# A mixture of experts inside a four-stage kernel: all experts for two blocks, and for six blocks rows sorted by expert and moved by indirect DMA

## The chip, the cores and the metric

The kernel runs on one core of a Trainium2 chip. The metric is the device time of one launch in microseconds. A core has a matrix engine (TensorE, PE in the profile; its weight loads are listed as PEld), a vector engine (VectorE, DVE), an activation engine (ScalarE, ACT), a general engine (GpSimd, POOL) and a queue that issues transfers (SyncE, SP). Each engine works through its own list of instructions in order.

## The reference

The input is four sequences of 1024 rows of 128 numbers. Four stages follow each other; each adds to `x` the layernorm of what it computed from the layernorm of `x`: a state-space scan ("mamba"), a mixture of experts, a windowed convolution whose 31 weights are computed per row and head, and a transformer of six layers with attention over windows of 32 rows. The stage that changes is the second:

```python
def _L0_ffn_ref(x, w_router, w_up, b_up, w_down, b_down):
    K = 2
    logits = jnp.einsum('bsd,ed->bse', x, w_router)
    top_logits, idx = jax.lax.top_k(logits, K)
    router_weights = jax.nn.softmax(top_logits, axis=-1)
    h = jnp.einsum('eud,bsd->bseu', w_up, x) + b_up[None, None]
    h = jax.nn.gelu(h, approximate=False)
    y = jnp.einsum('edu,bseu->bsed', w_down, h) + b_down[None, None]
    y_k = jnp.take_along_axis(y, idx[..., None], axis=2)
    out = jnp.einsum('bskd,bsk->bsd', y_k, router_weights)
    return out
```

There are eight experts of 512 hidden units. Every row needs only the two experts with the largest logits, a quarter of what the formula computes. Everything is in f32.

## The kernel before

The rows are worked in eight blocks of 512 (two to a sequence), `x[k]` for block k. `mamba(k)`, `moe(k)` and `conv(k)` prepare a block; the transformer takes a sequence in tiles of 128 rows, 4 sequences x 6 layers x 8 tiles = 192 tiles, numbered through.

`moe` (line 669) normalises a block, transposes it to `xT`, computes the logits, and finds the two best experts by reductions and comparisons on small tiles (`lg`, `hot`, `best`, `gates`), so that `gates` holds the weight of each of the eight experts, zero for six of them. Then it goes through 16 pairs of half a block and expert (`sub` outside, `e` inside). For each it loads the expert's up and down weights (`ewup`, `ewdn`, 256 KB each, from SP), multiplies up (`up`: four matmuls of 256 columns into two banks, Gelu by ACT), and one step later down (`down`: eight matmuls of 128 columns), multiplies the result by the gate (`eye`, DVE) and adds it to `eacc` (POOL). So all experts are computed for all rows, and the weights of a block are loaded twice.

The order of the instructions is made by the kernel itself. The stages are generators that record units of work (`Order.take`, line 164), with yields that say how much was recorded. `Transformer.run` (line 1268) records the tiles one after the other and, between their parts, advances two lines of side jobs: experts (lines 1295 and 1296) and others, mamba and conv (lines 1297 to 1300). An entry such as `(E, 3, 23, 36)` means the experts of block 3 are recorded from tile 23 to tile 36. Blocks 0 and 1 are recorded ahead of the transformer by `merge` (line 422). Then `Order.arrange` (line 267) gives out the units: for each engine it takes, among the units whose inputs its own table of durations (`length`, line 240) says are there, those that can start within a small margin (`NEAR`, line 147) and of them the one recorded first; it looks at most 500 units ahead and hands out seven PSUM banks. `Order.give` (line 344) issues them, which is why nearly every record of the profile has its line, L349. The hardware runs each engine's list in that order, with semaphores for what is not ready.

SP's list holds all transfers, POOL's none. On SP the rotary tables (`rot`, one per tile, three buffers), the transformer's weights and the expert weights follow each other. On POOL stand the rotary additions `r<-r,rb`, the multiplications `r<-r,root` and `at<-at,sm`, the adds of mamba and conv, and `eacc`.

Buffers are rings of a fixed number (`Rings`, line 379). Two that the change touches: `hs` (the transformer's state, two tiles `hs0` and `hs1`, each with two buffers, line 897) and `fxT` in `feedforward` (line 1218), which has its own buffer.

Of the kernel before, what the change touches and what calls it, by code (L numbers as in the profile page):

```python
# [24 lines left out]
NEXP, UP = 8, 512  # L25
NUC = UP // P
# [6 lines left out]
SUB = 256  # L33
# [23 lines left out]
class Late:  # L57
# [13 lines left out]
    def rearrange(self, *a, **k):  # L71
        return self.then(lambda ap: ap.rearrange(*a, **k))

# [66 lines left out]
class Order:  # L140
# [23 lines left out]
    def take(self, engine, op, args, kw):  # L164
        out = kw.get("out", args[0] if args else None)
        ins = [a for a in list(args) + list(kw.values()) if a is not out]
        ins = [a for a in ins if isinstance(a, (Late, bass.AP))]
# [72 lines left out]
    def length(self, engine, op, out, ins, kw):  # L240
# [17 lines left out]
        if engine == "scalar":  # L258
            return 0.25 + n * (0.45e-3 if n <= 512 else 0.7e-3), 0.12
        if op in ("tensor_copy", "memset"):  # L260
            return 0.15 + n * 1.0e-3, 0.08
# [139 lines left out]
@with_exitstack  # L401
def sandwich(ctx: ExitStack, tc: tile.TileContext, io: dict, out: bass.AP):


    c = Common(ctx, tc, io, out)
    t = Transformer(ctx, c)
    prepare = t.prepare()
    for _ in c.mamba(0):
        next(prepare, None)
    merge([(c.mamba(1), MAMBA), (c.moe(0), MOE), (prepare, 2.0 * DEPTH)])  # L410
    merge([(c.conv(0), CONV), (c.moe(1), MOE)])
    t.run()
    c.nc.arrange()
    with tc.manual_schedule():
        c.nc.give()
# [3 lines left out]
MAMBA, MOE, CONV = 60.0, 64.0, 59.0  # L419
# [15 lines left out]
class Common:  # L435


    def __init__(self, ctx, tc, io, out):
# [11 lines left out]
        self.rows = [dram.tile([PADL + SEQ, D], F32, name=f"rows{b}") for b in range(NB)]  # L450

# [18 lines left out]
        self.bup = const.tile([P, NEXP, NUC], F32, name="bup")  # L470
        self.bdn = const.tile([NEXP, D], F32, name="bdn")
        self.wl = const.tile([P, CH * CK], F32, name="wl")
        for t, k in (
# [5 lines left out]
            (self.bup, "b_upT"),  # L479
            (self.bdn, "b_dn"),  # L480
            (self.wl, "w_linT"),
        ):
# [15 lines left out]
        zero = const.tile([PADL, D], F32, name="zero")  # L498
        nc.gpsimd.memset(zero, 0.0)
        for rows in self.rows:  # L500
            dma(out=rows[:PADL, :], in_=zero)
# [167 lines left out]
    def moe(self, k):  # L669
        nc, dma, io = self.nc, self.dma, self.io  # L670
        x = self.x[k]
        full, row = [P, 4, NEXP], [P, 4]
        size = {
            "wup": ([P, UP], 2), "wdn": ([P, NUC, D], 3), "hg": ([P, 2, SUB], 4),
            "ye": ([P, 2, D], 2), "xT": ([P, BLK], 1), "acc": ([P, 4, D], 1),
            "gT": ([P, BLK], 1), "lg": (full, 1), "gates": (full, 1), "hot0": (full, 1),
            "hot1": (full, 1), "top": ([P, 2, 4], 1), "best": (row, 1), "ed": (row, 1),
            "wgt": ([P, 2, 4], 1),
        }

        def tile(name):
            shape, bufs = size[name]
            tag = "xn" if name == "gT" else name
            return self.sb.tile(shape, F32, name, tag="e" + tag, bufs=bufs)

        def weights(i):
            e = i % NEXP
            wup, wdn = tile("wup"), tile("wdn")
            dma(out=wup, in_=io["w_upT"][:, e, :])
            dma(out=wdn, in_=io["w_dnT"][:, e, :, :])  # L690
            return wup, wdn

        ahead = [weights(0)]
        xT = tile("xT")
        xn = self.norm(x, "e", "exn")
        yield 4
        nc.scalar.copy(xT, self.turned(xn, "e"))
        yield 2


        pl = self.bank("pl")[:, : 4 * NEXP].rearrange("p (t e) -> p t e", e=NEXP)
        with nc.together(0.9):
            for t in range(4):
                nc.tensor.matmul(
                    pl[:, t, :], xT[:, t * P : (t + 1) * P], self.wr, start=True, stop=True
                )
        lg, gates, top, best = tile("lg"), tile("gates"), tile("top"), tile("best")
        hot = [tile("hot0"), tile("hot1")]
        rank = self.rank[:, None, :].to_broadcast(full)
        nc.vector.tensor_copy(lg, pl)  # L710
        for i in range(2):
# [9 lines left out]
            if i == 0:  # L721
# [3 lines left out]
                nc.vector.tensor_tensor(out=lg, in0=lg, in1=gates, op=ALU.min)  # L725

        ed, wgt = tile("ed"), tile("wgt")
# [5 lines left out]
        for i in range(2):  # L733
            nc.vector.tensor_tensor(
                out=hot[i], in0=hot[i], in1=wgt[:, i, :, None].to_broadcast(full), op=ALU.mult
            )
        nc.vector.tensor_tensor(out=gates, in0=hot[0], in1=hot[1], op=ALU.add)
        yield 6


        acc = tile("acc")

        def biases():
            gT = tile("gT")
            ps = self.transpose4("gTp", [gates[:, g, :] for g in range(4)])
            nc.scalar.copy(gT[:NEXP], ps[:NEXP].rearrange("p g f -> p (g f)"))
            yield 2
            pa = self.bank("pacc").rearrange("p (g f) -> p g f", g=4)
            with nc.together(0.9):
                for g in range(4):  # L750
                    nc.tensor.matmul(
                        pa[:, g, :], gT[:NEXP, g * P : (g + 1) * P], self.bdn, start=True, stop=True
                    )
            nc.scalar.copy(acc, pa)
            yield 2

        def up(e, sub, wup):
            hg = []
            for i in range(NUC // 2):
                pu = self.bank("pu").rearrange("p (u f) -> p u f", u=2)  # L760
                h = tile("hg")
                with nc.together(0.88):
                    for u in range(2):
# [3 lines left out]
                            wup[:, uc * P : (uc + 1) * P],  # L767
# [706 lines left out]
```

## Time and profile before

| | |
|---|---|
| median of three runs | 4319.4 us (4319.16 to 4320.47) |
| profiled execution | 4318.73 us, its span 4316.9 us |
| mean granted TensorE clock | 0.965 |
| PE, DVE, ACT, POOL busy | 3947.9, 3714.9, 2672.7, 2867.3 us |
| DMA | 264.55 MB, mean 61 GB/s |
| expert weight loads | 256 of 256 KB |

A row of a group reads: line, engine, operation, output and input by the program's names, shapes, count, then the busy time and the mean of one record, then the idle time of the engine just before them and what ended most of it. Busy times of PE are unions of overlapping records, so the mean of one record is longer than its share of the busy time; an f32 matmul leaves two records, a transpose and a bf16 matmul one. The span falls into a start (0 to about 330 us, blocks 0 and 1 before the first transformer tile), a long middle in which transformer tiles and side jobs mix, and an end from about 3450 us in which the transformer is alone. The expert matmuls of blocks 2 to 7 lie between 648 and 3238 us.

### The profile page before, as it was taken

What the parts mean: (1) busy time and instruction counts of PE and PEld (TensorE: products, weight loads), DVE (VectorE), ACT (ScalarE), POOL (GpSimd) and SP (SyncE); (2) the same over time, 40 slices, a digit from 0 to 9 for tenths busy, and PEclk for the clock granted to TensorE, in tenths of its full rate; (3) what the DMA queues carried; (4) which work ended last, traced back from release to release, by engine and by line L of the source; (5) the groups of instructions that cost most, each with busy time, mean ns of one, the idle gap of its engine ahead of it and who ended that gap; (6) DMA issues with size and microseconds to landing.
All of it is one profiled execution on the core that took longest, in us unless ns stands there. A gap on an engine that the chain in (4) does not pass through costs nothing. (4 is left out here: it accounts for less than half of the span.)

```text
span 4316.9 us, 114247 instructions
## 1 busy us (share of the span) xinstructions
PE 3947.9 (91%) x46400; PEld 2883.0 (67%) x46400; DVE 3714.9 (86%) x9520; ACT 2672.7 (62%) x4666; POOL 2867.3 (66%) x1760
## 2 busy tenths in 40 slices
PE   5665789999999999899999999999999999999997
PEld 2553456776666777677766767677767677777775
DVE  5537799988899899998999989988889989989986
ACT  4443557666765676567756677566765566666664
POOL 4467656658668666696668666578558766666663
PEclk7887899999999999999999999999999999999999
DMA  5542001122112111121111211121111111001010
GB/s 173 193 151 83 28 29 37 62 80 92 60 65 75 48 52 50 57 92 56 47 60 66 68 44 44 63 82 53 54 63 56 46 33 34 30 24 34 25 34 11
DMA packets 127223, 264.55 MB, mean 61 GB/s; under 512 B 14384, under 2 KB 66792, under 8 KB 118760
## 3 DMA queue, kind: packets, MB, share of 16 engines
q1 hardware_dynamic: 126696, 257.25, 17.9%
q8 instruction: 365, 5.98, 0.6%
q14 instruction: 162, 1.33, 0.1%
HBM read 238.26 MB, written 18.94 MB: 60 GB/s over the span
## 5 line engine op out<-in xcount | busy, mean ns | idle before, releaser
L349 POOL TENSOR_TENSOR r<-r,rb 128x1024 f32<-128x1024 f32 x384 | 905.8, 2362 | 446.7 <-DVE rb L349 357.8
L349 POOL TENSOR_TENSOR r<-r,root 128x1024 f32<-128x1024 f32 x384 | 723.2, 1904 | 225.2 <-DVE root L349 192.2
L349 PEld LDWEIGHTS bank<-zT,wvo 128*128 128x128 f32 x6144 | 716.4, 192 | 100.2 <-issue 54.5
L349 PE MATMUL bank<-wqk,hs 128*128 128x512 f32 x1536 | 743.7, 614 | 33.9 <-DVE at L349 11.8
L349 PE MATMUL bank<-zT,wvo 128*128 128x128 f32 x6144 | 722.3, 276 | 9.8 <-ACT zT L349 6.9
L349 ACT ACTIVATE sq<-bank 128x512 f32<-128x512 f32 x768 | 439.7, 599 | 356.5 <-PE bank L349 133.1
L349 ACT COPY zT<-bank 128x512 f32<-128x512 f32 x768 | 401.0, 597 | 340.2 <-PE bank L349 339.5
L349 POOL TENSOR_TENSOR at<-at,sm 128x1024 f32<-128x1024 f32 x192 | 365.5, 1904 | 347.6 <-DVE sm L349 200.3
L349 DVE TENSOR_TENSOR r<-bank,rot 128x512 f32<-128x512 f32 x768 | 523.7, 682 | 74.3 <-PE bank L349 28.6
L349 DVE TENSOR_TENSOR rb<-bank,rot 128x512 f32<-128x512 f32 x768 | 524.3, 683 | 48.1 <-ACT sq L349 46.4
L349 DVE TENSOR_REDUCE words<-sq 128x8 f32<-128x512 f32 x768 | 527.6, 687 | 5.9
L349 PEld LDWEIGHTS bank<-wqk,hs 128*128 128x128 f32 x1536 | 273.8, 193 | 322.4 <-issue 191.5
L349 PE MATMUL bank<-ident,r 128*128 128x128 f32 x3072 | 394.5, 278 | 52.3 <-POOL r L349 18.3
L349 PE MATMUL bank<-aT,xw 64*128 64x256 f32 x3072 | 426.2, 399 | 16.7 <-DVE at L349 6.8
L349 PEld LDWEIGHTS bank<-ident,r 128*128 128x128 f32 x3072 | 349.5, 143 | 119.6 <-issue 43.3
L349 PEld LDWEIGHTS bank<-aT,xw 64*128 64x128 f32 x3072 | 296.1, 189 | 142.5 <-issue 54.4
L349 ACT ACT_TABLE_LOAD x264 | 338.7, 1283 | 28.0 <-DVE ne L349 10.4
L349 ACT COPY qT<-bank 128x512 f32<-128x512 f32 x384 | 228.1, 596 | 192.2 <-PE bank L349 188.7
L349 PEld LDWEIGHTS bank<-kT,qT 64*32 64x32 f32 x24576 | 254.9, 105 | 85.7 <-issue 83.1
L349 DVE TENSOR_REDUCE mx<-bank 128x8 f32<-128x512 f32 x384 | 254.2, 682 | 50.1 <-PE bank L349 49.8
L349 PE MATMUL bank<-exT,ewup 128*128 128x256 f32 x1024 | 270.3, 399 | 26.9 <-DVE near L349 11.0
L349 PE MATMUL bank<-kT,qT 64*32 64x64 f32 x24576 | 286.4, 226 | 0.6 <-issue 0.6
(148 smaller groups left out, 7155.5 us busy)
## 6 DMA issues: line engine op xcount, KB each, us to landing
ewup<-in_w_upT SPq DMA_DIRECT2D x128, 256.0 KB
ewdn<-in_w_dnT SPq DMA_DIRECT2D x128, 256.0 KB
near<-rows SPq DMA_DIRECT2D x32, 1024.0 KB
near<-rows SPq DMA_DIRECT2D x32, 960.0 KB
rot<-rotd SPq DMA_DIRECT2D x192, 128.0 KB
wqk<-in_Wqkv SPq DMA_DIRECT2D x48, 512.0 KB
wvo<-wvod SPq DMA_DIRECT2D x24, 1024.0 KB
w<-in_W SPq DMA_DIRECT2D x24, 341.0 KB
```

Of the source, the lines that this page charges most:

```text
L349: getattr(engine, op)(*map(real, args), **{k: real(v) for k, v in kw.items()})
```

## The change

Blocks 0 and 1 keep all experts, in `all_experts`: the expert outside and the half block inside, so that a weight tile is loaded once per block; up weights, down weights and the bias lie in one row of `w_ex` (4112 bytes per partition, 526 KB per expert), with three buffers and two loads ahead.

Blocks 2 to 7 are taken by sequence, two blocks at a time, in `chosen_experts`. After the same routing (now `route`, for one or two blocks), a matmul with a triangle of ones counts for every row how many earlier rows chose the same expert; from this follow each row's two places in a list sorted by expert, in which each expert begins at a multiple of 128, and the expert of each of the list's 23 tiles (16 full ones and up to seven part-filled). 16 indirect DMAs, issued by POOL, write the normalised rows to a DRAM list (`listed`); each list is zeroed once at the start. For each tile POOL fetches that expert's weights by an indirect DMA, SP loads the 128 rows; PE transposes them, multiplies up and down; ACT copies the result out and SP stores it to `results`. At the end POOL fetches each row's two results by indirect DMAs (16), and DVE adds them with their weights to the bias term, which stays in a PSUM bank. In the built program POOL so issues 48 scatters, 69 weight fetches and 48 gathers, each scatter waiting for the one before; ACT's list holds 173 table loads, before 264.

The side jobs are placed anew. `indirect_dma_start` gets an entry in the table of durations. To make room, `hs1` has one buffer, and `fxT` shares that of `fxn`.

```diff
-    merge([(c.mamba(1), MAMBA), (c.moe(0), MOE), (prepare, 2.0 * DEPTH)])
-    merge([(c.conv(0), CONV), (c.moe(1), MOE)])
+    merge([(c.mamba(1), MAMBA), (c.all_experts(0), ALL), (prepare, 2.0 * DEPTH)])
+    merge([(c.conv(0), CONV), (c.all_experts(1), ALL)])
...
+        for listed in self.listed:
+            dma(
+                out=listed.rearrange("(i p) d -> p i d", p=P),
+                in_=zero[:, None, :].to_broadcast([P, MAXT, D]),
+            )
...
+    def all_experts(self, k):
+        def weights(e):
+            w = self.sb.tile([P, 2 * UP + NUC], F32, "ewt", bufs=3)
+            dma(out=w, in_=self.io["w_ex"][e * P : (e + 1) * P, :])
+            return w
+        ahead = [weights(0), weights(1)]
...
         for i in range(2 * NEXP):
-            sub, e = divmod(i, NEXP)
+            e, sub = divmod(i, 2)
...
+    def chosen_experts(self, ks):
+        n = 4 * len(ks)
+        nt = 2 * n + NEXP - 1
...
+        yield from self.route(ks)
+        xn, _, lg, hot, gates, wgt = self.routed
+        nc.vector.tensor_tensor(out=hots, in0=hot[0], in1=hot[1], op=ALU.add)
...
+            nc.tensor.matmul(
+                count[:, :w], self.tri, flat, start=True, stop=False, skip_group_check=True
+            )
+            for t in range(1, n):
+                nc.tensor.matmul(
+                    count[:, t * NEXP : w],
+                    self.ones,
+                    flat[:, : w - t * NEXP],
...
+        for t in range(n):
+            for i in range(2):
+                nc.gpsimd.indirect_dma_start(
+                    out=listed[:, :],
+                    out_offset=at(idx[:, i, t : t + 1]),
+                    in_=xn[:, t, :],
+                    in_offset=None,
+                )
+                yield 1
+
+        def fetch(i):
+            w = self.sb.tile([P, 2 * UP + NUC], F32, "ewt", bufs=3)
+            nc.gpsimd.indirect_dma_start(
+                out=w, out_offset=None, in_=self.io["w_ex"], in_offset=at(widx[:, i : i + 1])
+            )
+            xs = self.sb.tile([P, D], F32, "exs", bufs=2)
+            dma(out=xs, in_=listed[i * P : (i + 1) * P, :])
+            return w, xs
+
+        def down(i, w, hg):
+            pd = self.bank("pdn")[:, :D]
...
+            ye = self.sb.tile([P, 2, D], F32, "ey", bufs=3)[:, 0, :]
+            nc.scalar.copy(ye, pd)
+            dma(out=results[i * P : (i + 1) * P, :], in_=ye)
+
+        ahead = [fetch(0), fetch(1)]
+        last = None
+        for i in range(nt):
+            w, xs = ahead.pop(0)
+            px = self.bank("pxs")[:, :P]
+            nc.tensor.transpose(px, xs, self.ident)
+            xT = self.sb.tile([P, P], F32, "exsT", bufs=2)
+            nc.scalar.copy(xT, px)
...
+            if last:
+                down(*last)
+            last = i, w, hg
+            if i + 2 < nt:
+                ahead.append(fetch(i + 2))
...
+        for i, k in enumerate(ks):
+            yield from self.biases(i, self.sb.tile([P, BLK], F32, "eT"), gates)
+            acc = self.biased
+            for g in range(4):
+                t = 4 * i + g
+                for j in range(2):
+                    yk = self.sb.tile([P, 2, D], F32, "ey", bufs=3)[:, 0, :]
+                    nc.gpsimd.indirect_dma_start(
+                        out=yk, out_offset=None, in_=results[:, :], in_offset=at(idx[:, j, t : t + 1])
+                    )
+                    nc.vector.scalar_tensor_tensor(
+                        acc[:, g, :], yk, wgt[:, j, t : t + 1], acc[:, g, :], ALU.mult, ALU.add
+                    )
+            yn = xn[:, :4, :]
+            self.layernorm(yn, acc, 4)
...
-                self.sb.tile([P, COLS], F32, f"hs{i}", bufs=2) for i in range(2)
+                self.sb.tile([P, COLS], F32, f"hs{i}", bufs=2 - i) for i in range(2)
...
-        xT = self.sb.tile([P, BLK], F32, "fxT")
+        xT = self.sb.tile([P, BLK], F32, "fxT", tag="fxn")
...
-        experts = [(E, 2, 10, 23), (E, 3, 23, 36), (E, 4, 36, 60), (E, 5, 60, 80)]
-        experts += [(E, 6, 80, 106), (E, 7, 106, 128)]
-        others = [(C, 1, 0, 2.6), (M, 2, 2.6, 10), (M, 3, 10, 20), (C, 2, 23, 30)]
-        others += [(M, 4, 30, 36), (C, 3, 36, 45), (M, 5, 46, 60), (C, 4, 60, 70)]
-        others += [(M, 6, 70, 80), (C, 5, 80, 93), (M, 7, 93, 106), (C, 6, 106, 124)]
-        others += [(C, 7, 128, 142)]
+        experts = [(E, (2, 3), 18, 30), (E, (4, 5), 56, 78), (E, (6, 7), 84, 118)]
+        others = [(C, 1, 0, 2.6), (M, 2, 2.6, 11), (M, 3, 11, 18), (M, 4, 18, 30)]
+        others += [(C, 2, 30, 38), (C, 3, 38, 46), (M, 5, 46, 56), (M, 6, 56, 67)]
+        others += [(M, 7, 67, 78), (C, 4, 78, 87), (C, 5, 87, 97), (C, 6, 118, 130)]
+        others += [(C, 7, 130, 144)]
```

## The prediction

> **What bounds the kernel now.** I read the totals first, then the busy times by stretch, then the groups of the stretch that the change touches, and then the waits. The totals say that two engines are nearly full together, TensorE before VectorE.
>
> ```profile
> span 4316.9 us, 114247 instructions
> ...
> PE 3947.9 (91%) x46400; PEld 2883.0 (67%) x46400; DVE 3714.9 (86%) x9520; ACT 2672.7 (62%) x4666; POOL 2867.3 (66%) x1760
> ...
> PE 3%; DVE 1%; ACT 0%; issue 0%; POOL 0%; POOLq 0%; ACTq 0%; DVEq 0%
> ```
>
> The chain that ended last reaches back only 4% of the span, so it covers the tail and says nothing about the middle. The stretches do (columns: stretch, length, then busy us and instruction count of PE, PEld, DVE, ACT, POOL; granted clock, DMA share, GB/s):
>
> ```profile
> 540.00:755.00 215.00, 196.78 (x2179) 136.03 (x2179) 203.02 (x491) 136.04 (x236) 135.02 (x85) 0.96 0.11 33
> 755.00:971.00 216.00, 208.68 (x2514) 161.62 (x2513) 190.73 (x493) 143.17 (x252) 128.74 (x83) 1.00 0.21 71
> ...
> 1187.00:1403.00 216.00, 197.87 (x2186) 140.12 (x2186) 203.38 (x512) 127.63 (x222) 156.66 (x91) 0.94 0.21 70
> ...
> 3454.00:4209.00 755.00, 748.82 (x10031) 549.70 (x10020) 682.21 (x1751) 462.74 (x806) 478.75 (x271) 1.00 0.10 30
> ```
>
> The last line is the transformer alone: PE 99%, a PE bound; 92 `mx` reductions, two a tile, lie in it, so 46 tiles at 16.4 us. The second has experts beside it: PE 97%, DVE 88%. The first and third have mamba and almost no experts: DVE 94%, PE 91.5%, clock 0.94 to 0.96, so there DVE is the fuller one. The six expert blocks that change all lie in 540 to 3200 us:
>
> ```profile
> 540.00:3200.00 2660.00, 2541.19 (x29806) 1866.20 (x29806) 2400.81 (x6137) 1771.73 (x3063) 1822.77 (x1123) 0.99 0.18 59
> ```
>
> In it PE is 95.5% busy and DVE 90.3%: together 1.858 of two engines. POOL has 837 us idle and ACT 888. Groups of that stretch (busy us, mean ns, then idle before them):
>
> ```profile
> L349 ACT ACT_TABLE_LOAD x206 | 264.3, 1283 | 24.2 <-DVE ne L349 10.4 <-DVE at L349 9.6 <-DVE rs L349 0.6
> L349 PE MATMUL bank<-exT,ewup 128*128 128x256 f32 x768 | 202.0, 392 | 9.3 <-DVE at L349 6.1 <-ACT zT L349 1.8 <-DVE hs L349 0.8
> L349 PE MATMUL bank<-ewdn,ehg 128*128 128x128 f32 x1536 | 191.1, 278 | 1.6 <-ACT ehg L349 1.2 <-DVE rb L349 0.4
> L349 ACT ACTIVATE ehg<-bank,bup 128x256 f32<-128x256 f32 x384 | 159.3, 477 | 53.6 <-PE bank L349 50.4 <-DVE mx L349 1.3
> ...
> L349 POOL TENSOR_TENSOR eacc<-eacc,eye 128x256 f32<-128x256 f32 x96 | 69.9, 728 | 45.8 <-DVE eye L349 24.8 <-DVE ne L349 13.1 <-DVE words L349 4.2
> L349 DVE TENSOR_TENSOR eye<-bank,egates 128x256 f32<-128x256 f32 x96 | 40.3, 420 | 37.1 <-PE bank L349 36.6
> ```
>
> The experts' matmuls hardly wait (9.3 and 1.6 us): they are work on a full engine, not latency. An f32 matmul leaves two records whose durations overlap, so I divide busy time by matmuls, not records: 191.1 / 768 = 0.249 us for one 128-column matmul.
>
> **The change, part by part (540 to 3200).**
> PE. Out go all eight experts of six blocks, 202.0 + 191.1 = 393 us. In come 3 groups x 23 tiles = 69 tiles of 128 rows: 8 matmuls of 128 columns and one transpose, 69 x (8 x 0.249 + 0.128) = 146 us (the transpose from the `ident,r` row, 394.5 us / 3072). The counting matmuls are new: 48 in bf16 of at most 64 columns; the nearest row is `near,sel`, 84.3 / 256 = 0.33 us for 512 columns. That bounds them at 16 us; I take 8. PE: -239 us.
>
> DVE. Out: 96 multiplications by the gates, 40.3 us. In: 48 accumulations of 128x128 from PSUM, between the `st` row (0.28) and the `fxn` row (0.40): 14 to 19. The final layernorm now reads PSUM, so 24 normalising steps come over from ACT at 0.404: 10. Routing runs three times for eight tiles instead of six times for four; its rows sum to 70 us, mostly waits of short instructions, so half to two thirds remain: -23 to -35. Counting and places: 14 short instructions a group, 4 to 8 us each group. Sum -40 + 14 + 10 - 25 + 17 = -24 us.
>
> ACT. Gelu 384 x 256 columns (159 us) becomes 276 x 128 columns. Halving a width saves about 0.09 us (the 512- and 256-column copies, 0.597 and 0.415, give 0.7 ns a column): 276 x 0.39 = 107; plus 138 copies x 0.32 = 44. The built order holds 173 table loads instead of 264: -91 x 1.283 = -117. ACT falls by about 125; it is not on the path, and shortens only latency.
>
> POOL. Out 69.9. In: 48 scatters, 69 weight fetches and 48 gathers, 165 DMAs issued by POOL itself, which no row shows. Bounds: the shortest POOL row of a tile (`kT` memset, 0.31 us) and the longest (2.36): 51 to 389 us. No row is near in kind. The Trainium skill, "DMA: Bandwidth & Descriptors", section "Latency and other measured facts", gives about 1 us to the first byte on this path; I take that as an estimate, 165 us. Even 389 fits in POOL's 837 idle us plus the 70 freed. What isn't hidden so surely is order: each scatter waits for the landing of the one before, each fetch for the down matmuls of three tiles earlier, each gather for its buffer. Behind them in POOL's queue stand the rotary adds (2.36), the `root` multiplications (1.90) and the attention weights (`at`), for which PE's transposes wait. In the built order one or two such operations mostly stand between two scatters, which covers a landing of 2 to 3 us; but eleven fetches of the first group stand within about one transformer tile.
>
> SP. 192 expert loads of the six blocks go; 69 row loads and 69 result stores of 64 KB come, in the same queue as the rotary tables. The first row load of a group waits for the last scatter; behind it stand `rot` tables (three buffers, a tile or more of lead, about 20 us). I cost it at nothing while a scatter chain is less late than that; beyond it, `project` starves.
>
> Data: 192 x 256 KB = 50 MB out, 69 x 526 KB, 138 x 64 KB on SP and 96 x 64 KB on POOL, about 52 MB, in: no relief. The DMA engines are 18% busy, so the amount costs nothing; eleven fetches in 20 us would ask for 290 GB/s, and 200 GB/s at a 57% share is the busiest 100 us of the trace (200 to 300). By it a fetch takes at least 1.5 us of bandwidth.
>
> Start (blocks 0 and 1, all experts): same PE work, expert outside and half outside-in, weights once. PE waits there for `ewup` 4.6 us in all; 3 MB of zero rows are added to SP. -5 to +15; I take 0. The shared buffers (`fxT` in `fxn`, one `hs1`) are next written some four tiles after their last reader: nothing. The accumulator holds one of seven banks during eight gathers; not costed.
>
> **A rule against it.** The egates row is the one place where the trace shows POOL and DVE in each other's way:
>
> ```profile
> L349 DVE TENSOR_SCALAR egates<-egates x8: 117/464/1762, 98.1 to 2785.3; 128x32 f32<-128x32 f32 x8
> ```
>
> Minimum, median and maximum ns of the same 32 elements: up to 1.6 us of waiting. The Trainium skill, "SBUF — State Buffer", section "SBUF: two separate sides", says more: while VectorE copies SBUF to SBUF in its two-port mode, POOL cannot write DMA descriptors, and a 620 ns DMA took about 3100. By the rule, with a DVE at 90%, each of the 165 would lose 2.5 us: 409 us of POOL stall, enough to turn the result. By the rows it is far less: nearly all DVE time here (`r`, `rb`, `words`, `at`, `mx`, scans) reads or writes PSUM or reduces, and SBUF-to-SBUF scalar or copy forms like the one above are a few dozen instructions. I go by the rows, and leave the rule to the slower rival.
>
> **The sum.** If PE were freed and nothing else bound, 239 / 0.955 = 250 us would go. But DVE loses only 24: at its best, 95 to 96% (203.02 of 215 is 94.4), 2377 us need 2476 to 2502, so DVE allows at most 158 to 184. The two wait for each other, so I let the joint share stay at 1.858, which also holds in the mamba stretch (1.860): (2541 - 239 + 2401 - 24) / 1.858 = 2518, -142 us. Two costs go on top. PE at 2302 / 2518 = 91% will be granted less clock: at that share the stretches show 0.94 to 0.96 against 0.99 now. At 0.96 PE's busy time grows by 72 us, 39 at the joint share; I take half, 20, since where DVE is the bound the clock costs nothing. Hand-overs of three groups (last scatter to first row load, last store to first gather): 10. So -112: span 4316.9 - 112 = 4205; the profiled execution took 4318.73, 1.8 more than its span: 4206.7; the median is 0.7 above the profiled run: **4207 us**.
>
> **Rivals.**
> 1. DVE gives way. Much of its busy time may be waiting for POOL's port, and fewer table loads shorten ACT's answers. Then the gain lies between DVE's floor (-184) and PE's (-250): about 4110. For it: the spread of the egates row. Against: the large rows (`r`, `rb`, `mx`) sit at 0.68 with no spread to lose.
> 2. POOL's in-order waits eat most of it: 165 waits at 0.5 us that PE feels are 82 us: 4290. For it: POOL's `r` and `at` already wait on DVE and are followed by PE. Against: POOL has slack.
> 3. Slower. The place is the weight fetch: PE's queue holds the tile's up matmuls in order, and everything of the transformer behind them. If a fetch (descriptors, 0.5 MB, semaphore) lands later than the two tiles of lead, PE stands still. It decides at 112 / 69 = 1.6 us per fetch; at 2.4 us, 166 lost, the time is about 4370 with the POOL stalls of the same fetches. The rule above is what would cause it.
> 4. The expert work was hidden anyway and nothing moves. Only if DVE bound everywhere; PE's 97 to 99% beside experts speaks against it.
>
> **How the numbers follow.** Chances: forecast 0.52 (own range 4155 to 4260), rival 1 0.16, rival 2 0.15, rival 3 0.14, rival 4 0.03. Faster by over 0.2% (about what a measurement of this kernel can tell from no change): 0.52 + 0.16 + 0.15 = 0.83; within 0.2% 0.03; slower 0.14. The range 4110 to 4320 leaves out half of rival 1 and rival 3.
>
> **What would show it.** Expert matmuls in the main stretch about 146 us of PE instead of 393; PE busy total near 3710 to 3780; DVE total within 40 us of 3715 and, in span share, now at PE's level (88% or more); ACT busy near 2550; 264 table loads down to 173. PE's idle before `exsT,ewt` should be small; idle of over 100 us there ended by the fetch means rival 3. POOL idle before `r`, `at` grown by over 80 us means rival 2. The transformer-alone stretch must keep its 16.4 us a tile. The forecast is wrong if POOL's DMA takes over 2.4 us to issue, or if DVE busy itself moves by over 60 us.

## The result, and the profile after

The changed kernel takes 4286.1 us (median of four, 4285.1 to 4286.8), beside 4319.5 for the kernel before: a ratio of 0.9922, 95% interval 0.9905 to 0.9939. It is 33 us faster. The forecast was 4207, 112 us faster: the sign is right, and under a third of the gain came. (The 4286 coincides with rival 2's 4290; its trace marks did not appear, as told below.)

The totals of the profiled execution, kernel after:

```profile
span 4284.5 us, 111840 instructions
...
PE 3811.2 (89%) x45298; PEld 2728.5 (64%) x45317; DVE 3661.2 (85%) x9478; ACT 2491.0 (58%) x4572; POOL 2965.3 (69%) x1826
```

PE lost 136.7 us of work and DVE 53.7, yet both are now busy for a smaller share of a shorter span. The groups of the experts, kernel after, whole run (busy us, mean ns, then idle before them and what ended it):

```profile
L357 ACT ACT_TABLE_LOAD x173 | 222.0, 1283 | 14.8 <-DVE at L357 10.3 <-PEq L1680 0.7 <-DVE cxT L357 0.5
L357 PE MATMUL bank<-ewt,ehg 128*128 128x128 f32 x1064 | 141.3, 284 | 4.2 <-DVE rb L357 1.9 <-ACT ehg L357 1.3 <-DVE ne L357 0.9
...
L357 PE MATMUL bank<-exsT,ewt 128*128 128x128 f32 x552 | 76.4, 283 | 7.9 <-DMA ewt<-in_w_ex,ewidx 2.5 <-ACT exsT L357 1.7 <-DVE cxT L357 1.5
...
L357 POOL DMA_INDIRECT ewt<-in_w_ex,ewidx x69 | 67.7, 981 | 43.0 <-PE bank L357 18.3 <-ACT ey L357 10.3 <-ACT exsT L357 4.8
...
L357 POOL DMA_INDIRECT listed<-exn,eidx x48 | 48.2, 1004 | 20.9 <-DMA listed<-exn,eidx 8.6 <-issue 5.5 <-DVE ne L357 4.6
L357 POOL DMA_INDIRECT ey<-results,eidx x48 | 46.5, 970 | 14.4 <-DVE words L357 3.7 <-issue 3.6 <-DVE ne L357 2.2
...
L357 PE MATMUL bank<-ident,exs 128*128 128x128 f32 x69 | 20.1, 301 | 31.5 <-DMA exs<-listed 27.8 <-DVE rs L357 1.3 <-DVE root L357 0.9
```

The prices of the parts nearly stand. 552 records (276 matmuls) on each side of the six blocks' tiles are 76.4 us up and 141.3 x 552/1064 = 73 us down, 150 of matmul where 137 were put; the 69 transposes took 20 where 9 were put, the counting 2 where 8 were. POOL issues an indirect DMA in 0.97 to 1.00 us, whether it carries 64 KB or 526 KB (514 in the profile's KB): 162 us for 165 of them. What PE waits for is not the weights (2.5 us) but the rows (27.8 us), nearly all in one place. The longest waits of PE, ACT and DVE (total us, times, longest), kernel after, 2443 to 2480 us:

```profile
PE bank L357 <- DMA exs<-listed: 26.8, 1, 26.8
ACT exsT L357 <- PE bank L357: 26.0, 1, 26.0
DVE rb L357 <- POOL r L357: 14.3, 2, 12.0
```

And the same place in the timeline (start, length, engine, operation):

```profile
2448.55 2.84 PE L357 MATMUL bank<-wqk,hs 128*128 128x512 f32 x6 [0.53 <-DVE rb L357]
2478.24 0.45 PE L357 MATMUL bank<-ident,exs 128*128 128x128 f32 x1 [26.84 <-DMA exs<-listed]
```

This is the start of the third group: PE's next instruction is the transpose of the first tile's rows, and it waits for the last of 16 scatters. What holds these up is mostly POOL's other work, which stands between them in its list. Busy times of the same place, columns as in the prediction:

```profile
2443.00:2478.00 35.00, 7.80 (x40) 5.00 (x40) 16.97 (x41) 2.88 (x6) 31.31 (x20) 0.67 0.30 106
```

POOL is 89% busy there, PE 22% and DVE 48%; POOL waits once for a landing in it, 2.8 us. A second place is the first group. Busy times by stretch, kernel after, same columns (the transformer alone; a mamba stretch; the middle of the first group):

```profile
3420.00:4175.00 755.00, 747.19 (x9959) 548.41 (x9959) 684.47 (x1762) 463.97 (x812) 483.33 (x271) 1.00 0.10 30
643.00:750.00 107.00, 93.56 (x1109) 62.06 (x1111) 104.41 (x240) 62.55 (x103) 74.22 (x48) 0.96 0.07 20
...
964.00:1071.00 107.00, 101.44 (x1034) 82.21 (x1037) 65.99 (x126) 69.93 (x184) 58.33 (x43) 0.97 0.37 112
```

At 964 to 1071 us PE is 95% busy and DVE 62%: once the rows are there, the tiles held up behind them come in one burst, and DVE has little to do. At 643 to 750 DVE is 97.6% busy. The transformer alone is as it was. So the two engines are filled at different times. To put a number on it, the whole stretch from the first `sm<-at` reduction of tile 0 to that of tile 144, kernel before and then kernel after:

```profile
367.00:3489.00 3122.00, 2922.69 (x34576) 2130.98 (x34574) 2790.43 (x7115) 2017.39 (x3495) 2178.13 (x1323) 0.98 0.18 58
```

```profile
361.00:3451.00 3090.00, 2789.71 (x33468) 1978.72 (x33484) 2732.31 (x7072) 1838.46 (x3402) 2274.29 (x1385) 0.96 0.18 59
```

The joint share of PE and DVE was (2922.69 + 2790.43) / 3122 = 1.830 and is (2789.71 + 2732.31) / 3090 = 1.787. Had it stayed, the 5522 us of work would have taken 5522 / 1.830 = 3017.5, 72 us less than they do. (The start, put at nothing, gained 6 us: tile 0 comes at 361 and not at 367.) The experiments ask what lowered the joint share.

### The profile page after: what moved, and what is told of

It reads as the page before. It is cut to its first block, busy times and chain, and to the rows that moved or that the text cites. A ratio compares the mean times of both kernels' runs of the same rounds, so it can differ in the third digit from the quotient of the medians.

```text
span 4284.5 us, 111840 instructions
## 1 busy us (share of the span) xinstructions
PE 3811.2 (89%) x45298; PEld 2728.5 (64%) x45317; DVE 3661.2 (85%) x9478; ACT 2491.0 (58%) x4572; POOL 2965.3 (69%) x1826
## 5 line engine op out<-in xcount | busy, mean ns | idle before, releaser
L357 POOL TENSOR_TENSOR r<-r,rb 128x1024 f32<-128x1024 f32 x384 | 908.2, 2373 | 370.9 <-DVE rb L357 304.7
L357 PE MATMUL bank<-wqk,hs 128*128 128x512 f32 x1536 | 771.0, 627 | 65.8 <-DVE at L357 33.2
L357 PE MATMUL bank<-zT,wvo 128*128 128x128 f32 x6144 | 731.8, 278 | 9.8 <-ACT zT L357 8.1
L357 DVE TENSOR_TENSOR r<-bank,rot 128x512 f32<-128x512 f32 x768 | 522.2, 680 | 83.6 <-PE bank L357 38.9
L357 DVE TENSOR_TENSOR rb<-bank,rot 128x512 f32<-128x512 f32 x768 | 519.8, 678 | 49.1 <-ACT sq L357 34.6
L357 PE MATMUL bank<-aT,xw 64*128 64x256 f32 x3072 | 440.6, 406 | 24.5 <-DVE near L357 7.0
L357 PE MATMUL bank<-ident,r 128*128 128x128 f32 x3072 | 403.8, 281 | 45.8 <-POOL r L357 23.6
L357 PE MATMUL bank<-fxn,w 128*128 128x512 f32 (+1 forms) x576 | 278.1, 612 | 8.7 <-ACT fxn L357 5.5
L357 ACT ACTIVATE at<-at 128x1024 f32<-128x1024 f32 x192 | 203.1, 1058 | 119.3 <-DVE at L357 85.5
```

Source lines behind the costliest of these rows:

```text
L357: getattr(engine, op)(*map(real, args), **{k: real(v) for k, v in kw.items()})
```

## Experiments

Three theories. *List*: freeing PE is worth what was forecast, and the list's machinery (scatters, fetches, gathers, its hand-overs) gives it back. *Places*: the new tiles of mamba, conv and experts give it back. *Floor*: DVE or the clock binds, and freeing PE is worth little by any means. Later the list was split into the landing waits of the scatters, POOL's time, the trips of the rows, and the form of the work. Each time is a median; runs of the kernel before beside them took 4320.7 to 4323.0.

**1. The relief without list or new places.** In the kernel before:

```diff
-        for i in range(2 * NEXP):
-            sub, e = divmod(i, NEXP)
...
+        used = NEXP if k < 2 else 3
...
+        for i in range(2 * used):
+            sub, e = divmod(i, used)
```

(and the constant that sets the pace at which these blocks are recorded, to 36)

> The kernel before, in its old placement and with its old direct weight loads, but blocks 2 to 7 compute only experts 0, 1 and 2 of the eight (the five others' share of the sum is left out). It takes 5/8 of the six blocks' expert matmuls away (246 us of PE, about what the list takes away), 25 us of DVE and 44 us of POOL, with no list, no scatter and no new order of the stages. Theory A (the relief is worth what I forecast, and the list or the order of the stages gave it back): 4170 to 4215, that is 105 to 150 below before. Theory B (DVE is the floor and the clock eats the rest, so the relief itself is worth little whatever the method): 4265 to 4295.

4219.8 us, ratio 0.9764 (0.9748 to 0.978): 102 us gained, 3 short of the 105 to 150 expected if the relief is worth its forecast, and far above the 26 to 56 of a floor. Floor falls. Freeing 246 us of PE is worth about what the forecast took it for.

**2. The new places with the old method.** In the kernel before, with all eight experts:

```diff
-        experts = [(E, 2, 10, 23), (E, 3, 23, 36), (E, 4, 36, 60), (E, 5, 60, 80)]
-        experts += [(E, 6, 80, 106), (E, 7, 106, 128)]
+        experts = [(E, 2, 18, 24), (E, 3, 24, 30), (E, 4, 56, 67), (E, 5, 67, 78)]
+        experts += [(E, 6, 84, 101), (E, 7, 101, 118)]
```

(and the others as in the changed kernel)

> The kernel before, all eight experts and direct loads, only with mamba, conv and experts at the tiles of the changed kernel (experts 2 and 3 at 18 to 24 and 24 to 30, and so on). Theory A1 (the new places themselves cost: experts and mamba are no longer beside what fills the other engine): 4345 to 4400, 25 to 80 above before. Theory A2 (the list's chain costs, the places do not): within 15 of before, 4305 to 4335. Theory B (DVE floor): within 15 of before.

4378.8, ratio 1.0141 (1.0124 to 1.0157): 57 us slower, so Places looked right. The next runs show that this holds only for the old amount of expert work.

**3. The changed kernel with plain transfers.**

```diff
-                nc.gpsimd.indirect_dma_start(
-                    out=listed[:, :],
-                    out_offset=at(idx[:, i, t : t + 1]),
...
+                r = (2 * t + i) * P
+                dma(out=listed[r : r + P, :], in_=xn[:, t, :])
...
-            nc.gpsimd.indirect_dma_start(
-                out=w, out_offset=None, in_=self.io["w_ex"], in_offset=at(widx[:, i : i + 1])
-            )
+            dma(out=w, in_=self.io["w_ex"][i // 3 * P : (i // 3 + 1) * P, :])
...
-                    nc.gpsimd.indirect_dma_start(
-                        out=yk, out_offset=None, in_=results[:, :], in_offset=at(idx[:, j, t : t + 1])
-                    )
+                    r = (2 * t + j) * P
+                    dma(out=yk, in_=results[r : r + P, :])
```

> The changed kernel with every indirect transfer of the six blocks replaced by a direct one of the same size on SP at fixed rows (three tiles each of experts 0 to 6 and two of expert 7; rows in their own order, results of the first sixteen tiles): which rows meet which expert is no longer right, the amount of every engine's work is, but POOL issues none of the 165 DMAs. Theory A2 (POOL's DMAs and the serial chain of scatters hold the rest up): 4205 to 4240, 45 to 80 below the changed kernel. Theory A1 (places): 4265 to 4285, 0 to 20 below it. Theory B: within 10 of it.

4231.3, ratio 0.9793 (0.9776 to 0.9809): 55 us below the changed kernel. With plain transfers, 55 of the 79 us that were missing (4286.1 against 4207) come back.

**4. Mamba of block 4 beside the burst.**

```diff
-        others = [(C, 1, 0, 2.6), (M, 2, 2.6, 11), (M, 3, 11, 18), (M, 4, 18, 30)]
-        others += [(C, 2, 30, 38), (C, 3, 38, 46), (M, 5, 46, 56), (M, 6, 56, 67)]
+        others = [(C, 1, 0, 2.6), (M, 2, 2.6, 11), (M, 3, 11, 18), (M, 4, 23, 32)]
+        others += [(C, 2, 32, 39), (C, 3, 39, 46), (M, 5, 46, 56), (M, 6, 56, 67)]
```

> The changed kernel with one stage moved: mamba of block 4 at tiles 23 to 32 in place of 18 to 30, so that it runs beside the first group's expert tiles (which in the trace come at tiles 26 to 30, after the scatters) and not beside its routing and scatters; conv of blocks 2 and 3 follow at 32 to 39 and 39 to 46. Theory A1 (experts alone beside the transformer fill PE and starve DVE, which is 52% busy at 945 to 1025 us): 20 to 45 below the changed kernel, 4240 to 4265. Theory A2 and theory B: within 10 of it.

4315.4, ratio 0.9985 (0.9978 to 0.9992): 29 us slower than the changed kernel, a miss. The burst stayed and starved DVE as before. Busy times over 60 us of the first group, first in this run, then in the kernel after:

```profile
930.00:990.00 60.00, 48.60 (x440) 41.90 (x439) 21.06 (x50) 37.42 (x103) 23.25 (x20) 0.91 0.46 141
```

```profile
945.00:1005.00 60.00, 52.37 (x471) 43.54 (x471) 23.88 (x63) 41.41 (x113) 28.78 (x24) 0.94 0.52 161
```

DVE is 35% and 40% busy. Moving mamba beside the experts didn't feed DVE there.

**5 and 6. Plain scatters only; plain fetches only** (each one of the three edits of run 3).

> The changed kernel with only the 48 scatters replaced by direct stores of the same 64 KB from SP, to rows in their own order (so the list is not sorted by expert); fetches of weights and gathers of results stay indirect on POOL. Stores to rows of their own don't wait for one another. Theory chain (the 16 scatters of a group follow one another, each waiting for the landing of the one before, and the first row load and PE's first transpose stand behind the last): it regains most of the 55 us that replacing all transfers did, 4235 to 4255, and PE's wait of 26.8 us for the first row load of group 3 is gone. Theory issue (each of the 165 POOL DMAs costs its share): 48/165 of 55 us, 4265 to 4275.

> The changed kernel with only the 69 fetches of weights replaced by direct loads of the same 526 KB from SP at a fixed expert (three tiles each of experts 0 to 6, two of expert 7; so most rows meet another expert than their own); scatters and gathers stay indirect on POOL. Theory chain: within 12 us of the changed kernel, 4274 to 4298, PE's long wait for the first row load of a group still there. Theory issue: 69/165 of 55 us or more, 4255 to 4268.

Scatters: 4235.8, ratio 0.9805 (0.9789 to 0.9822), 50 below the changed kernel. Fetches: 4270.8, ratio 0.9884 (0.9868 to 0.9901), 15 below it and between the two expectations; PE's wait for the rows stays (26.9 us). So 48 of the 165 DMAs carry nearly all of the 55; the parts don't add up exactly (50 and 15 are more than 55), and each edit also lets the kernel's planner lay out another order.

**7. Three of eight at the new places** (runs 1 and 2 together).

> Three of eight experts without any list (as in the first experiment, five experts of the six blocks left out), now with mamba, conv and experts at the tiles of the changed kernel. What it takes over the 4219.8 of the old places is the price of the places at the changed kernel's load. If the 57 us that the places cost with all eight experts come from too much expert work in few tiles, it shrinks with that work to 3/8 or less: 4220 to 4240, and what the changed kernel takes above this is the list's. If the places cost by themselves (mamba and conv on each other's heels): 4260 to 4280.

4194.2, ratio 0.9700 (0.9683 to 0.9716): 127 us gained, 26 more than at the old places, below what either reading expected. Places falls: with little expert work the new places are the better ones. This is the yardstick for the list: the same places, nearly the same work, no list (and the buffers and the start of the kernel before). Its stretch from tile 0 to tile 144:

```profile
367.00:3371.00 3004.00, 2751.11 (x33151) 1951.62 (x33150) 2743.70 (x7065) 1809.18 (x3172) 2134.73 (x1263) 0.97 0.15 50
```

Joint share (2751.11 + 2743.70) / 3004 = 1.829: that of the kernel before. The list, with all that came along with it, therefore costs 4286.1 - 4194.2 = 92 us. In the profiles 87 of them lie between tile 0 and tile 144: 72 are the lower joint share, 15 are more work (5522.0 against 5494.8, at 1.83).

**8. One block to a list, at the old places** (`(E, (2,), 10, 23)` and so on, six groups, with the pace constant to match).

> The changed kernel's method with one block to a list and not two, at the tiles of the old kernel (experts of block 2 at 10 to 23 and so on): six lists of 15 tiles, 90 tiles in place of 69 (42 us more of expert matmuls), chains of 8 scatters in place of 16. If the chain's length and the burst after it are what the list costs, halved chains and the old places cost little, and only the 21 more tiles are paid at about 0.4 us per us of work, 4255 to 4285. If each hand-over has its price whatever its length, six in place of three: 4300 to 4330.

4338.8, ratio 1.0040 (1.0026 to 1.0054). Halved chains did not help; six lists cost more than three, as the second reading had it and a little beyond. Slower than both kernels.

**9. Plain scatters, but issued by POOL.**

```diff
-                nc.gpsimd.indirect_dma_start(
-                    out=listed[:, :],
-                    out_offset=at(idx[:, i, t : t + 1]),
...
+                r = (2 * t + i) * P
+                nc.gpsimd.dma_start(out=listed[r : r + P, :], in_=xn[:, t, :])
```

(and an entry for such a DMA in the planner's table of durations)

> As the run with plain scatters (direct stores to rows in their own order, so the list is not sorted), but issued by POOL as the indirect ones are: POOL pays for 16 issues a group and keeps their places in its order, only the wait of each for the landing of the one before is gone, since they write rows of their own. Theory landing (the serial waits make the cost): like the plain stores from SP, 4235 to 4255. Theory POOL time (16 issues a group beside conv, where POOL is 84% busy at tiles 87 to 97): little is regained, 4270 to 4288.

4265.4, ratio 0.9865 (0.9848 to 0.9881): between the two, 21 below the changed kernel and 30 above the plain scatters from SP. Neither theory alone. One tile's view of this run, and the same of the kernel after, says what changed for POOL (ns, minimum, median, maximum):

```profile
L359 POOL DMA_DIRECT2D listed<-exn x48: 537/555/807, 800.2 to 2443.8; - x48
```

```profile
L357 POOL DMA_INDIRECT listed<-exn,eidx x48: 969/1000/1207, 863.5 to 2474.1; - x48
```

A plain DMA also costs POOL 0.45 us less, 21 us in all, so the 21 gained are the landing waits and part of POOL's price together. The other 30 go only when the scatters leave POOL's list, in which they stand among the work that PE and DVE wait for. How much of the 30 is issue time (48 x 0.555 = 27 us, if all of it is felt) and how much the place in the list, this run does not part. In the changed kernel POOL itself stood still for a landing in 5 of 48 cases, 8.6 us in all. Instead the planner puts other work, mostly one to three instructions, between two scatters, and from the first to the last of a group's 16 it takes 66, 74 and 81 us.

**10. Each scatter twice.**

```diff
-                nc.gpsimd.indirect_dma_start(
-                    out=listed[:, :],
...
+                for _ in range(2):
+                    nc.gpsimd.indirect_dma_start(
+                        out=listed[:, :],
...
```

> The changed kernel with each of the 48 scatters issued twice in a row to the same rows; the list is the same. A group's chain has 32 links in place of 16. Theory landing: at least as much again as the scatters cost now (50 us), more where cover runs out, 4335 to 4405. Theory POOL time alone (48 more issues of 1.0 us on an engine 69% busy): 4290 to 4310. If the scatters lie beside other work: within 10 us of the changed kernel.

4378.4, ratio 1.0130 (1.0114 to 1.0147): 92 us slower than the changed kernel for 48 more scatters, 1.9 us each, as the landing theory had it. Waits of PE in this run (total us, times, longest):

```profile
PE bank L357 <- DMA exs<-listed: 63.4, 8, 45.7
```

The chain is on the path, and the second 48 links cost more than the first 48, at 50 us.

**11. The third group earlier.**

```diff
-        experts = [(E, (2, 3), 18, 30), (E, (4, 5), 56, 78), (E, (6, 7), 84, 118)]
+        experts = [(E, (2, 3), 18, 30), (E, (4, 5), 56, 78), (E, (6, 7), 79, 118)]
```

> The changed kernel with one number changed: experts of blocks 6 and 7 begin at tile 79 in place of 84 (mamba of block 7 ends at 78), still to 118, so that the 16 scatters lie beside conv of block 4 and the start of that of block 5, and the first row load is due earlier than its first use. Theory landing: PE's 26.8 us before the first transpose of group 3 go, 4256 to 4272. If that wait only stands for another engine that was late (POOL with conv), the wait moves and the time stays within 8 us, 4278 to 4294.

4277.9, ratio 0.9900 (0.9884 to 0.9917): 8 us below, with an interval that overlaps the changed kernel's, hence undecided between nothing and a little. The wait itself went (waits of PE in this run):

```profile
PE bank L357 <- DMA exs<-listed: 1.4, 2, 0.7
```

So the most striking line of the profile (the start apart), 26.8 us of PE standing still, was worth 8 at most. By the tiles, this run is 38 us behind the changed kernel at tile 84, 11 ahead at tile 97 and 1 ahead at tile 144; the rest of the 8 comes where the transformer is alone. The time is lost while the group is routed and counted, before the first scatter at 2314 us, and not beside the scatters. Busy times of this run before and beside the scatters:

```profile
2281.00:2319.00 38.00, 15.40 (x181) 8.94 (x181) 34.13 (x107) 7.26 (x14) 27.58 (x16) 0.63 0.18 60
2319.00:2400.00 81.00, 76.74 (x957) 57.32 (x955) 67.70 (x178) 50.34 (x94) 67.36 (x48) 0.97 0.27 92
```

In the first PE is 41% busy and waits for DVE, which is 90% busy; in the second PE is 95% busy. Removing the wait moved the delay; it did not remove it.

**12. The stages placed with the chains in mind.**

```diff
-        experts = [(E, (2, 3), 18, 30), (E, (4, 5), 56, 78), (E, (6, 7), 84, 118)]
...
+        experts = [(E, (2, 3), 19, 30), (E, (4, 5), 56, 78), (E, (6, 7), 81, 114)]
+        others = [(C, 1, 0, 2.6), (M, 2, 2.6, 12), (M, 3, 12, 18), (M, 4, 18, 30), (C, 2, 30, 40), (C, 3, 40, 46), (M, 5, 46, 55), (M, 6, 55, 67), (M, 7, 67, 78), (C, 4, 78, 89), (C, 5, 89, 98), (C, 6, 115, 130), (C, 7, 130, 144)]
```

> The changed kernel with its stages placed with the chains in mind and nothing else changed: experts of (2, 3) at 19 to 30 and (6, 7) at 81 to 114; mamba 2 to 12 and 3 to 18, 5 at 46 to 55, 6 at 55 to 67; conv 2 at 30 to 40, 3 at 40 to 46, 4 at 78 to 89, 5 at 89 to 98, 6 at 115 to 130. If the list's loss is where and beside what the chains fall, most of the 50 us that plain scatters regained can be had with the true ones: 4235 to 4260, below both kernels. If a hand-over has a fixed price wherever it stands: within 12 us of the changed kernel.

4266.9, ratio 0.9877 (0.9860 to 0.9893), the interval wholly below the changed kernel's: 19 us better than it and 56 than the runs of the kernel before beside it. The fastest that computes everything, but short of the 26 to 51 expected: most of the list's price stays at these places too.

**13. No trips of the rows.** Run 3 with

```diff
-                dma(out=listed[r : r + P, :], in_=xn[:, t, :])
...
-            dma(out=xs, in_=listed[i * P : (i + 1) * P, :])
-            return w, xs
+            return w, xn[:, i % n, :]
...
-            dma(out=results[i * P : (i + 1) * P, :], in_=ye)
...
-                    dma(out=yk, in_=results[r : r + P, :])
+                    yk = xn[:, t, :]
```

> The run with plain transfers, and the rows' trips through DRAM left out as well: a tile's rows are taken from the normalised block in SBUF, nothing is stored to the list or to the results, and the sums at the end add rows of that block in place of results; the experts' weights still come by direct loads. Every instruction of PE, DVE and ACT stays, 170 transfers of 64 KB on SP go. Theory trips: most of the 37 us above three of eight at the same places go, 4195 to 4212. Theory form (tiles of 128 rows): within 10 us of plain transfers, 4221 to 4241.

4231.5, ratio 0.9788 (0.9772 to 0.9805): equal to plain transfers (4231.3). The trips through DRAM cost nothing as long as no indirect DMA is in them. What remains over three of eight, 37 us, is neither the indirect DMAs nor the trips. The first candidate is the form of the work: tiles of 128 rows, with routing, counting and the sum for two blocks at once. The one buffer of `hs1`, the shared one of `fxT` and the new start also differ between the two kernels and were not tried by themselves; against them speaks the table below, where plain transfers lose to three of eight 9, 6 and 20 us in the stretches with a list and nothing outside them, though the shared buffers hold everywhere. Stretch from tile 0 to tile 144 of run 13:

```profile
363.00:3401.00 3038.00, 2766.60 (x33486) 1968.61 (x33486) 2740.02 (x7073) 1841.81 (x3407) 2110.84 (x1221) 0.97 0.17 55
```

Work 5506.6 against 5494.8 of run 7, 12 us more, 6 us at 1.83; the rest is a joint share of 1.813 in place of 1.829. Which part lowers it (more and shorter instructions from bank to copy to matmul, three PSUM banks for 128 rows in place of 256, the bank held for the sum) was not tried.

Where the list's price falls, by the starts of the `sm<-at` reductions in the traces (us from tile to tile):

| tiles | changed | scatters twice | plain scatters, POOL | plain scatters, SP | all plain | three of eight, same places |
|---|---|---|---|---|---|---|
| 18 to 30 (group 1) | 315 | 370 | 311 | 301 | 289 | 280 |
| 56 to 78 (group 2) | 499 | 526 | 496 | 491 | 492 | 486 |
| 78 to 118 (group 3) | 817 | 827 | 806 | 794 | 787 | 767 |
| 0 to 144 | 3091 | 3180 | 3069 | 3043 | 3038 | 3004 |

Between the changed kernel and three of eight, the stretches with a list make 35, 14 and 50 us (before rounding); what lies between them is 12 the other way. Plain scatters from SP take back 14, 8 and 23 of these. That is most in group 3, where conv of blocks 4 and 5 stands beside the chain, and conv puts much on POOL (263.5 us of the run in `near<-near,ew` alone). But run 10 does not bear this out: there the second 48 scatters cost 55, 27 and 10 us, most in group 1, beside mamba, where 11 of the last 13 links follow each other with nothing between them in POOL's list, and least beside conv. What the price of a place depends on is therefore open; conv was not tried by itself.

## Why the prediction was wrong in size

**The relief: right.** -142 at the joint share and +20 for the clock made -122 without the hand-overs. The same relief without a list gained 102 at the old places and 127 at the new ones, and the joint share held (1.823 and 1.829 beside 1.830). The method of the sum, two nearly full engines whose joint share stays, is borne out for a change that only takes work away. The two parts of that sum erred and partly cancelled: in run 7 PE's busy time from tile 0 to 144 fell by 172 us and not by the 246 taken out, DVE's by 47 and not by 25.

**The step that failed** is the last term, "Hand-overs of three groups (last scatter to first row load, last store to first gather): 10", together with POOL's 165 us that were held to be hidden because "Even 389 fits in POOL's 837 idle us plus the 70 freed", so that the joint share was left as it was. The list costs 92. About 50 are the 48 scatters, shown by taking them off POOL's list; of these some 30 remain when they are plain and free of each other but still issued by POOL, and 21 go with the landing waits and the shorter issue. Some 5 more come with fetches and gathers (fetches alone 15). The last 37 have no indirect DMA in them: probably the tiles' form, which the sum priced as PE work and not as a cause of waits. The idle time was there; but here an idle sum over a stage did not tell what happens in an in-order list in which 16 links of 1.0 us and 2.3 us of landing alternate with additions and multiplications that PE and DVE wait for. The share of the sum was therefore not 1.858, nor the 1.830 of the whole stretch, but 1.787: 72 us.

**The terms of work** make up the rest: PE fell by 137 and DVE by 54 over the run, 191 in place of 227 (263 less the 36 granted to the clock); at 1.83 that is 20 us. The 36 missing are 17 of expert work and 49 of slower matmuls, less 30 that DVE gave beyond its forecast. The expert matmuls fell by 222 over the whole run (526.1 before, 270.3 + 255.8; 304.6 after, transposes and counts included) instead of 239, and groups that didn't change grew: `wqk,hs` from 743.7 to 771.0, `aT,xw` from 426.2 to 440.6, and so on, 85 in all. I took half of 72 for the clock; the mean granted clock fell from 0.965 to 0.946, and no less than the 72 came. The price of a transpose was too low as well: 0.128 us was read from a row of 3072 that follow each other, and one by itself took 20.1 / 69 = 0.29. DVE, forecast at -24, gave 54.

**Rival 1** (DVE gives way) did not come: DVE's large rows took what they took before (`r<-bank,rot` 523.7 and 522.2 us, `rb<-bank,rot` 524.3 and 519.8), and the 54 us that DVE lost are work that left. Its sign, the spread of the `egates` row, is real but small: the three longest of the eight (1.04, 1.45 and 1.76 us) each end 34 to 41 ns after a POOL instruction does. **Rival 2** gave the right time by waits on POOL, and its place, POOL's in-order list, was the right one; but its mark was wrong. I looked for idle POOL before `r` and `at`; idle before `r<-r,rb`, for one, fell from 446.7 to 370.9 us (before, then after):

```profile
L349 POOL TENSOR_TENSOR r<-r,rb 128x1024 f32<-128x1024 f32 x384 | 905.8, 2362 | 446.7 <-DVE rb L349 357.8 <-PE bank L349 34.8 <-DVE ne L349 31.6
```

```profile
L357 POOL TENSOR_TENSOR r<-r,rb 128x1024 f32<-128x1024 f32 x384 | 908.2, 2373 | 370.9 <-DVE rb L357 304.7
```

Where POOL is late, POOL isn't idle: the idleness is on PE and DVE, as at 2443 to 2478 us. That the time came near rival 2's is luck: it put 165 waits at 0.5 us each, and 48 scatters made most of it. **Rival 3** fell by the fetches: 2.5 us of wait. The rule of the Trainium skill that was set against the change ("SBUF — State Buffer", section "SBUF: two separate sides"), by whose example a POOL DMA would lose some 2.5 us to VectorE, did not show: in 165 issues the longest took 1.21 us, and half of the scatters landed within 2.3 us of their issue, the quickest in 2.2. Of the 48, 11 took over 3 us to land; the slowest, 6.4 us, was issued at 2451 us, where loads from SP kept the DMA engines 78 and 88% busy (2448 to 2451, 2451 to 2454 us). So the mean DMA share of 18%, by which the prediction held the amount of data to cost nothing, is no bound for a place like this; what delayed the others was not looked into. Going by the rows was right, and so was the estimate of 1 us an issue (162 us in place of 165), with some luck: the figure it was taken from is the time to the first byte, not the time that POOL is held. **Rival 4** fell with run 1. Among the stated marks, table loads (173) and the stretch of the transformer alone came as put, and the wait before `exsT,ewt` was small (7.9 us). The expert matmuls came near (172 us with transposes and counting, put at 154), ACT fell further than put (2491, put near 2550). PE's total (3811, put at 3710 to 3780) and DVE's 88% of the span (85%) did not come: the first says that less PE time went than was taken out, the second that the joint share fell.

**Still open:** what costs the 37 (a part of the tiles' form, or the shared buffers), and how much of each step of ten or so us between runs is the planner's other order and not the edit. Run 4 and run 11 moved 29 and 8 us by moves of stages alone, so parts under ten us are not told apart here.

## What to carry to other kernels

Price a relief by leaving the work out and nothing else, and the machinery that achieves it by the difference to that run: here the relief was worth 127 us and the list took 92 of them. An engine with idle time can still be on the path when its list is in order and a serial chain is put into it; ask which engines wait for the work that the chain is mixed with. The longest wait in a trace is a place to look, not a sum to collect: taking it away, 26.8 us, gave 8 at most.

## What was not expected of the hardware

An indirect DMA cost POOL 0.96 to 1.00 us at the median whether each partition moved 512 bytes or 4112; a plain one of 64 KB, in run 9, cost it 0.555 and landed in 1.8. From issue to landing, the medians were 2.3 us (scatter), 2.5 (gather) and 4.4 (fetch of 526 KB), the same kernel, after:

```profile
L357 POOL DMA_INDIRECT ewt<-in_w_ex,ewidx x69: 936/982/1033, 865.0 to 2855.3; - x69
...
DMA to landing us min/median/max: 4.0/4.4/8.3
```

And the clock: with PE at 90% of the stretch from tile 0 to tile 144 and not 94%, the granted clock there fell from 0.98 to 0.96, and the six largest groups of unchanged matmuls took 1 to 4% more busy time over the run, so that over a third of the PE time taken out came back (85 of 222 us). That this is the clock and not, in part, the other order is read from the granted clock alone.
